# Three-block transformer layer on one core: the first attention's units one step further apart, with q, k and v copied to SBUF and norms made tile by tile

## The chip, the cores and the metric

The kernel runs on one NeuronCore of a Trainium2 chip. The core has a matrix engine (TensorE, PE in the profile), a vector engine (VectorE, DVE), an activation engine (ScalarE, ACT), a general engine (GpSimd, POOL), a queue that only starts transfers (SyncE, SP), and 16 DMA engines. SBUF is its working memory of 128 partitions; PSUM is the small memory that TensorE writes its results to, in 8 banks. Each engine runs its own instructions in order, and semaphores tie the engines together. The metric is the device time of one execution in microseconds.

## The reference

The input x has 8 batches of 512 tokens with 256 features. Four residual blocks follow one another, each on a normalised x:

```python
x = x + attn_a(layernorm(x))      # 16 heads of 64
x = x + ffn(layernorm(x))
x = x + attn_b(layernorm(x))      # 16 heads of 16, causal over the 512 tokens
x = x + ffn(layernorm(x))         # the same weights again
```

`attn_a` is unusual: it attends among the 64 channels of one head of one token, not among tokens.

```python
Q = (x @ Wq + bq).reshape(b, s, H, C) / 8;  K, V likewise
scores = einsum('bshq,bshk->bshqk', Q, K)       # 64 x 64 per token and head, causal
attn = einsum('bshqk,bshk->bshq', softmax(scores), V)
return attn.reshape(b, s, 1024) @ Wo + bo
```

So each of 4096 tokens has 16 matrices of 64 x 64 that are outer products: work for elementwise engines, not for TensorE. The FFN is silu(x W1) * (x W2), then two gelu layers of 1024, then a projection to 256; its weights are whole numbers with a scale for each output.

## The kernel before

**Groups and units.** `AttentionA` handles a group at a time: a batch b, a set g of four heads, and a tile i of 128 tokens (one token on each partition). There are 8 x 4 x 4 = 128 groups. The causal triangle of a 64 x 64 matrix is cut into squares of side 32, 16, 8, 4, 2 and 1 and the diagonal. `units` (line 549) collects the squares of a group into four units: the two heads' squares of side 32 twice, all of side 16, and all the small ones. So the first attention has 512 units, and `step(n)` (line 633) works on several at a time, each at another stage:

- `scores` (706) multiplies q by k. POOL does it for the two units of side 32, in two instructions of 1024 columns each, reading q and k from SBUF; DVE does it for the others and for the diagonal, reading q from PSUM and k from SBUF.
- `exps` (722) is the exponential on ScalarE.
- `weigh` (733) multiplies the exponentials by v on DVE, with v in PSUM, and has POOL's queue issue a DMA that adds one half of the tile to the other (line 744).
- `fold` (746) is another addition on POOL, for side 32, and the sums of the smallest squares.
- `gather` (760) reduces the rest on DVE, and POOL adds the result to `acc` (`add_rows`, 776), which holds denominators and numerators.
- `divide` (781), `turn_group` (786) and `project_out` (796) finish a group and add it to x.

Here `weigh` works on the unit of one step before `scores`, `fold` on that of two, `gather` of three steps before. Four tiles of 16 KB per partition (`wt`) carry the units. `project` (680) makes q, k and v with TensorE, two steps ahead; k and q are copied to SBUF (lines 690 and 700), and q and v stay in the two banks of `ps_qv` until the group ends.

**The rest of the layer.** `after_a` (1192) is a generator that emits FFN, second attention and FFN of a batch. Its pieces are woven into the steps of the next batch's first attention: each step emits pieces until their estimated cost has caught up (`total`, line 1235, and the loop at 1244). So the first batch's first attention has little beside it, and the last batch's remaining blocks run alone. The kernel fixes the order on PE, DVE, ScalarE and POOL itself, by the order in which it emits (`manual_schedule`). `later` and `flush` put an emission off to the next point of the same generator.

**Normalisation.** `stats` (509) takes mean and variance of several tiles on DVE, the square root on ScalarE, its reciprocal and the shift on DVE (lines 519 and 524). `normed` scales on ScalarE, and `turned_over` transposes on TensorE. For the blocks after the first attention `Normed` does three of the four tiles together and the last one later. In the FFN, line 932 takes the difference between a product and its rounded copy on POOL. In the last FFN, `fits` compares the weights with their rounded copies on DVE (line 909).

**Buffers.** `hp` has 8 blocks of 8 KB for activations, `wp` two buffers for the projection weights, which SP's queue loads, `ps_a` one bank for the first attention's other products, `ps_f` five banks for all the rest.

Of the kernel before, what the change touches and what calls it, by code (L numbers as in the profile page):

```python
# [284 lines left out]
def fast_path(ctx: ExitStack, tc: tile.TileContext, k, t, flag):  # L285

    nc = tc.nc
    ident, eps = k.ident, k.eps
# [3 lines left out]
    wp = ctx.enter_context(tc.tile_pool(name="wp", bufs=2))  # L292
# [5 lines left out]
    hp = ctx.enter_context(tc.tile_pool(name="hp", bufs=8))  # L298
    small = ctx.enter_context(tc.tile_pool(name="small", bufs=3))
    ps_qv = ctx.enter_context(tc.tile_pool(name="ps_qv", bufs=2, space=bass.MemoryType.PSUM))  # L300
    ps_a = ctx.enter_context(tc.tile_pool(name="ps_a", bufs=1, space=bass.MemoryType.PSUM))
# [24 lines left out]
    for g in range(NG):  # L326
        if g < 2:

            wqv = wp.tile([P, DC, 2 * GW], F32, tag="wqv", name=f"wqv_0_{g}")
            wk = wp.tile([P, DC, GW], F32, tag="wk", name=f"wk_0_{g}")  # L330
        else:
            both = block(f"fit_{g}")
            wqv = both[:, : DC * 2 * GW].rearrange("p (c f) -> p c f", c=DC)
            wk = both[:, DC * 2 * GW : DC * 3 * GW].rearrange("p (c f) -> p c f", c=DC)
        nc.sync.dma_start(wqv, wqv_r[:, :, g, :])
        nc.sync.dma_start(wk, wk_r[:, :, g * GW : (g + 1) * GW])
        fitted.append((wqv, wk))
# [171 lines left out]
    def stats(b, xt, part, tiles=range(NT)):  # L509

        i0, i1 = tiles[0], tiles[-1] + 1
        mv = small.tile([P, NT, 2], F32, tag=f"mv_{part}", name="mv", bufs=2)[:, i0:i1]
        for i in tiles:
            st = small.tile([P, 6], F32, tag=f"st_{part}", name="st")
            nc.vector.bn_stats(st, xt[:, i, :])
            nc.vector.bn_aggr(mv[:, i - i0, :], st)
        rstd = small.tile([P, NT], F32, tag=f"rstd_{part}", name="rstd", bufs=2)[:, i0:i1]
        nc.scalar.activation(rstd, mv[:, :, 1], AF.Sqrt, bias=eps)
        nc.vector.reciprocal(rstd, rstd)
        if part == "f":  # L520
            shift = small.tile([P, NT], F32, tag="shift", name="shift", bufs=2)[:, i0:i1]
        else:
            shift = means[:, b, 0 if part == "a" else 1, i0:i1]
        nc.vector.scalar_tensor_tensor(shift, mv[:, :, 0], -1.0, rstd, ALU.mult, ALU.mult)
        return {i: (rstd[:, i - i0 : i - i0 + 1], shift[:, i - i0 : i - i0 + 1]) for i in tiles}

    def normed(xi, rn, part):

        rstd, shift = rn
# [9 lines left out]
    def turned_over(dst, xn, pool):  # L539
# [4 lines left out]
        nc.scalar.copy(dst, pt)  # L544
# [4 lines left out]
    units = (((32, 0, 2),), ((32, 2, 2),), ((16, 0, 4),), ((8, 0, 4), (4, 0, 4), (2, 0, 4), (1, 0, 4)))  # L549
    NU = len(units)  # L550

# [10 lines left out]
    def pieces(w, n, off, nsq, cols):  # L562
# [11 lines left out]
        if n < 16:  # L574
            e, ev = (
                w[:, a * 2048 + off : a * 2048 + off + nsq * n * n].rearrange("p (x i j) -> p x i j", i=n, j=n)
# [22 lines left out]
    class AttentionA:  # L599
# [3 lines left out]
        def __init__(self):  # L603
            self.x = {0: x_first}
            self.rn, self.live = {}, {}
            self.w = {(0, g): fitted[g] for g in range(2)}
            self.wo = {}
            self.load_wo(0, 0)
            self.ready = set()
# [3 lines left out]
            self.steps = len(self.todo) + 11  # L613
# [10 lines left out]
        def load_wo(self, b, g):  # L624
            if b < NB:
                wo = wp.tile([P, GW // P, D], F32, tag="wo", name=f"wo_{b}_{g}", bufs=1)
                nc.sync.dma_start(wo, t.wo[g * GW : (g + 1) * GW].rearrange("(c p) f -> p c f", p=P))
                self.wo[b, g] = wo
# [4 lines left out]
        def step(self, n):  # L633
            b, i, g, u = self.at(n)
            if b is not None:
                self.scores(b, i, g, u)
            b, i, g, u = self.at(n + 40)
            if u == 0 and g == 0 and i == 0 and b > 0:
                self.x[b] = load_x(b)
            b, i, g, u = self.at(n + 7)  # L640
            if u == 0 and g == 0 and i == 0:
                self.rn[b] = stats(b, self.x[b], "a")
            b, i, g, u = self.at(n + 4)
            if u == 0 and g == 0:
                self.norm(b, i)
            yield
            b, i, g, u = self.at(n - 1)
            if b is not None:
                self.weigh(b, i, g, u)
            b, i, g, u = self.at(n - 2)  # L650
            if b is not None:
                self.fold(b, i, g, u)
            b, i, g, u = self.at(n + 2)
            if u == 0:
                self.project(b, i, g)
            yield
            b, i, g, u = self.at(n - 3)
            if b is not None:
                self.gather(b, i, g, u)

            b, i, g, u = self.at(n - 4)
            if u == NU - 1:
                self.divide(b, i, g)
            b, i, g, u = self.at(n - 8)
            if u == NU - 1:
                self.turn_group(b, i, g)
            b, i, g, u = self.at(n - 9)
            if u == NU - 1:
                self.project_out(b, i, g)
            yield  # L670
            b, i, g, u = self.at(n)
            if b is not None:
                self.exps(b, i, g, u)

        def norm(self, b, i):
            xnt = lnp.tile([P, DC, P], F32, tag="xnt_a", name=f"xnta_{b}_{i}", bufs=NT)
            turned_over(xnt, normed(self.x[b][:, i, :], self.rn[b][i], "a"), ps_a)
            self.live[b, i] = xnt

        def project(self, b, i, g):  # L680
# [8 lines left out]
            kt = ap_.tile([P, 2, GW], F32, tag="k", name=f"k_{u}")  # L689
            nc.scalar.copy(kt[:, 0], pk)  # L690
            qv = ps_qv.tile([P, 2, GW], F32, tag="qv", name=f"qv_{u}")
            for c in range(DC):
                nc.tensor.matmul(  # L693
                    qv.rearrange("p j f -> p (j f)"),
                    xnt[:, c, :],
                    wqv[:, c, :],
                    start=(c == 0),
                    stop=(c == DC - 1),
                )
            nc.scalar.copy(kt[:, 1], qv[:, 0])  # L700
            acc = ap_.tile([P, 2, GW], F32, tag="acc", name=f"acc_{u}", bufs=4)
            self.live[b, i, g] = (qv, kt, acc)
            if i == 1 and (b, g) != (0, 0):
                self.load_w(b + (g + 1) // NG, (g + 1) % NG)

        def scores(self, b, i, g, n_u):

            qv, kt, acc = self.live[b, i, g]
            w = wt.tile([P, 4096], F32, tag="w", name=f"w_{b}_{i}_{g}_{n_u}")
            self.live[b, i, g, n_u] = w  # L710
            if n_u == 0:
                nc.vector.tensor_tensor(acc[:, 0, :], qv[:, 0, :], kt[:, 0], ALU.mult)
            for n, off, nsq, cols in squares(units[n_u]):

                eng, q = (nc.gpsimd, kt[:, 1]) if n_u < 2 else (nc.vector, qv[:, 0])
                for e, ev, rows, columns in pieces(w, n, off, nsq, cols):
                    shape = list(e.shape)
                    eng.tensor_tensor(  # L718
                        e, rows(q).to_broadcast(shape), columns(kt[:, 0]).to_broadcast(shape), ALU.mult
                    )  # L720

        def exps(self, b, i, g, n_u):
            qv, kt, acc = self.live[b, i, g]
            w = self.live[b, i, g, n_u]
            if n_u == 0:
                nc.scalar.activation(acc[:, 0, :], acc[:, 0, :], AF.Exp, scale=C**-0.5)
            if n_u < 3:
                e = w.rearrange("p (b a r) -> p a b r", a=2, b=units[n_u][0][0] // JB)[:, 0]
            else:
                e = w[:, : sum(nsq * n * n for n, off, nsq, cols in squares(units[n_u]))]  # L730
            nc.scalar.activation(e, e, AF.Exp, scale=C**-0.5)  # L731

        def weigh(self, b, i, g, n_u):


            qv, kt, acc = self.live[b, i, g]
            w = self.live[b, i, g, n_u]
            if n_u == 0:
                nc.vector.tensor_tensor(acc[:, 1, :], acc[:, 0, :], qv[:, 1, :], ALU.mult)
            for n, off, nsq, cols in squares(units[n_u]):  # L740
                for e, ev, rows, columns in pieces(w, n, off, nsq, cols):
                    nc.vector.tensor_tensor(ev, e, columns(qv[:, 1]).to_broadcast(list(e.shape)), ALU.mult)  # L742
            if n_u < 3:
                nc.gpsimd.dma_start(w[:, :2048], w[:, 2048:], accum_op=ALU.add)  # L744

        def fold(self, b, i, g, n_u):

            qv, kt, acc = self.live[b, i, g]
            w = self.live[b, i, g, n_u]
            for n, off, nsq, cols in squares(units[n_u]):  # L750
                if n == 32:
                    nc.gpsimd.tensor_tensor(w[:, :1024], w[:, :1024], w[:, 1024:2048], ALU.add)  # L752
                if n <= 2:
                    both = w.rearrange("p (a f) -> p a f", a=2)[:, :, off : off + nsq * n * n]
                    both = both.rearrange("p a (r j) -> p a r j", j=n)
                    if n == 2:
                        nc.gpsimd.tensor_tensor(both[..., :1], both[..., :1], both[..., 1:], ALU.add)
                    self.add_rows(acc, n, cols, both[..., 0])

        def gather(self, b, i, g, n_u):  # L760

            qv, kt, acc = self.live[b, i, g]
            w = self.live.pop((b, i, g, n_u))
            for n, off, nsq, cols in squares(units[n_u]):
                if n <= 2:
                    continue
                if n >= 16:
                    both = w[:, : 2 * nsq * n * JB].rearrange("p (a r j) -> p a r j", a=2, j=JB)
                else:
                    both = w.rearrange("p (a f) -> p a f", a=2)[:, :, off : off + nsq * n * n]  # L770
                    both = both.rearrange("p a (r j) -> p a r j", j=n)
                red = ap_.tile([P, 2, nsq * n], F32, tag=f"red{nsq * n}", name=f"red_{b}_{i}_{g}_{n_u}_{n}")
                nc.vector.tensor_reduce(red, both, AX.X, ALU.add)  # L773
                self.add_rows(acc, n, cols, red)

        def add_rows(self, acc, n, cols, part):

            rows = acc[:, :, cols].rearrange("p a (x t) -> p a x t", t=2 * n)[..., n:]
            nc.gpsimd.tensor_tensor(rows, rows, part.rearrange("p a (x i) -> p a x i", i=n), ALU.add)  # L779

        def divide(self, b, i, g):
            qv, kt, acc = self.live[b, i, g]
            nc.vector.reciprocal(acc[:, 0, :], acc[:, 0, :])
# [555 lines left out]
```

## Time and profile before

| what | value |
|---|---|
| median of 3 runs | 4479.16 us (4476.88 to 4479.33) |
| the profiled execution | 4477.29 us, its span 4475.5 us |
| granted clock of TensorE, mean | 0.806 |
| ScalarE, exponentials of 2048 columns (line 731) | 384, mean 1914 ns |
| DVE, reductions of 2048 columns (line 773) | 256, mean 2277 ns |
| POOL, folds (line 752) | 256, mean 2594 ns |
| DMA, the adding transfer (line 744) | 384 of 1024 KB, 7.2 us from issue to landing |
| from 4200 us to the end | PE busy 249.8 of 275 us, DVE 82.7, POOL 31.9 |

Busy shares are means over the whole span, and the last batch's end differs from the rest. In a row of a group, the first number after the bar is its busy time in us, the second the mean of one instruction in ns, and what follows the second bar is the idle time of the engine just before these instructions, with what ended it. An instruction's duration runs from its start on the engine to its end: what it waits for on a semaphore lies outside of it, what holds it after its start lies within.

### The profile page before, as it was taken

Reading aid. Unit: us, or ns where it says so; the run is one execution under the profiler, and the core shown is the slowest. Engines: PE = TensorE matmul, PEld = TensorE weight load, DVE = VectorE, ACT = ScalarE, POOL = GpSimd, SP = SyncE. Lnnn points to the kernel's source line nnn. Section 1 sums busy time; section 2 is a strip of 40 time slices with the busy share of each in tenths; the row PEclk is TensorE's granted clock in tenths of the full one; section 3 lists DMA queues with packets and bytes.
Section 4 is the critical chain, followed back from the end, with each engine's and each line's share of the span. In section 5 each row is a group of like instructions: output and inputs, shape, how many; then the busy total and the mean of one; then the engine's idle time right before and its main releaser. Section 6 shows DMA issues by size and latency. Waiting matters only on the chain. (4 is left out here: it accounts for less than half of the span.)

```text
span 4475.5 us, 37073 instructions
## 1 busy us (share of the span) xinstructions
PE 2959.5 (66%) x11880; PEld 2017.9 (45%) x11880; DVE 3511.3 (78%) x4113; ACT 2422.0 (54%) x3068; POOL 2962.6 (66%) x2634
## 2 busy tenths in 40 slices
PE   3322277567865777757875678657777568756998
PEld 2111154245633555335642456335553356425757
DVE  5988877888888888878878788888888788787205
ACT  3333365565754765556654666547655566546332
POOL 6777776766776776767767667667767677676201
PEclk6555588788987889878987889778898789878999
DMA  7555566657755767647765577557676477655514
GB/s 234 124 123 119 123 163 168 124 140 178 192 125 111 181 165 176 134 112 177 178 168 124 139 177 198 119 111 182 161 178 133 110 180 172 168 115 135 180 43 147
DMA packets 118364, 670.24 MB, mean 150 GB/s; under 512 B 12672, under 2 KB 31883, under 8 KB 43536
## 3 DMA queue, kind: packets, MB, share of 16 engines
q0 software_dynamic: 78336, 570.46, 56.3%
q1 hardware_dynamic: 39824, 97.32, 6.3%
q8 instruction: 96, 1.57, 0.1%
q14 instruction: 108, 0.88, 0.1%
HBM read 255.12 MB, written 9.96 MB: 59 GB/s over the span
## 5 line engine op out<-in xcount | busy, mean ns | idle before, releaser
L742 DVE TENSOR_TENSOR w<-w,qv 128x1024 f32<-128x1024 f32 (+3 forms) x1280 | 1198.7, 985 | 443.5 <-ACT w L731 443.5
L731 ACT ACTIVATE w<-w 128x2048 f32<-128x2048 f32 (+1 forms) x512 | 966.0, 1887 | 842.0 <-POOL w L718 560.8
L1016 PE MATMUL ph<-h,hidden 128*128 128x512 f32 x4096 | 1095.3, 424 | 158.4 <-POOL h L932 90.4
L773 DVE TENSOR_REDUCE red<-w 128x128 f32<-128x1024 f32 (+2 forms) x640 | 1036.6, 1636 | 23.9 <-POOL w L752 19.1
L718 POOL TENSOR_TENSOR w<-k 128x1024 f32<-128x1024 f32 x512 | 1036.2, 2136 | 7.6 <-ACT k L700 7.4
L1016 PEld LDWEIGHTS ph<-h,hidden 128*128 128x128 f32 x4096 | 819.7, 203 | 386.9 <-POOL h L932 113.7
L744 POOL DMA_DIRECT2D w<-w x384 | 334.8, 872 | 979.1 <-DVE w L742 331.4
L752 POOL TENSOR_TENSOR w<-w 128x1024 f32<-128x1024 f32 x256 | 664.1, 2594 | 64.6 <-DMA w<-w 64.2
L718 DVE TENSOR_TENSOR w<-qv,k 128x1024 f32<-128x1024 f32 (+3 forms) x768 | 601.5, 838 | 6.9
L779 POOL TENSOR_TENSOR acc<-acc,red 128x256 f32<-128x256 f32 (+1 forms) x640 | 473.1, 739 | 139.5 <-DVE red L773 121.0
L948 PE MATMUL pw<-xnt,gate 128*128 128x512 f32 (+2 forms) x1152 | 328.7, 439 | 166.8 <-ACT silu L927 84.6
L543 PE MATMUL ps_ln<-ident,xn 128*128 128x128 f32 x256 | 76.5, 415 | 488.7 <-ACT xn L536 330.6
L1126 PE MATMUL pyb<-eb,vb 128*32 128x512 f32 (+3 forms) x1024 | 219.6, 525 | 255.7 <-ACT eb L1121 255.5
L948 PEld LDWEIGHTS pw<-xnt,gate 128*128 128x128 f32 x1152 | 236.6, 225 | 244.9 <-ACT silu L927 101.8
L686 PE MATMUL pk<-wk,xnta 128*128 128x256 f32 x512 | 191.6, 512 | 196.6 <-DVE x L808 195.2
L693 PE MATMUL qv<-wqv,xnta 128*128 128x512 f32 x512 | 288.0, 692 | 0.0
L543 PEld LDWEIGHTS ps_ln<-ident,xn 128*128 128x128 f32 x256 | 37.3, 193 | 529.7 <-ACT xn L536 353.7
L1041 PE MATMUL pof<-w,h 128*128 128x256 f32 x1024 | 244.9, 399 | 12.5 <-ACT h L981 12.5
L981 ACT ACTIVATE h<-ph,s_sb 128x512 fp32r<-128x512 f32 (+1 forms) x256 | 172.2, 688 | 129.7 <-PE ph L1016 128.4
L1126 PEld LDWEIGHTS pyb<-eb,vb 128*32 128x32 f32 x1024 | 66.2, 117 | 362.2 <-ACT eb L1121 336.5
L686 PEld LDWEIGHTS pk<-wk,xnta 128*128 128x128 f32 x512 | 124.1, 258 | 231.4 <-DVE x L808 206.3
L1041 PEld LDWEIGHTS pof<-w,h 128*128 128x128 f32 x1024 | 204.4, 202 | 48.0 <-ACT h L981 17.3
(130 smaller groups left out, 4196.5 us busy)
## 6 DMA issues: line engine op xcount, KB each, us to landing
w<-w POOLq DMA_DIRECT2D x384, 1024.0 KB, 7.2
hidden<-in_h POOLq DMA_DIRECT2D x128, 1024.0 KB, 6.6
gate<-in_w12p POOLq DMA_DIRECT2D x32, 1024.0 KB, 5.7
w<-w_d SPq DMA_DIRECT2D x16, 1024.0 KB
wqv<-wqv_d SPq DMA_DIRECT2D x30, 512.0 KB, 3.1
wo<-in_wo SPq DMA_DIRECT2D x32, 256.0 KB, 6.6
wbqk<-wbqk_d SPq DMA_DIRECT2D x8, 1024.0 KB
w<-in_h SPq DMA_DIRECT2D x8, 1024.0 KB, 8.5
```

The lines of the kernel that those rows point to most:

```text
L686: nc.tensor.matmul(pk, xnt[:, c, :], wk[:, c, :], start=(c == 0), stop=(c == DC - 1))
L693: nc.tensor.matmul(qv.rearrange("p j f -> p (j f)"), xnt[:, c, :], wqv[:, c, :], start=(c == 0), stop=(c == DC - 1),)
L718: eng.tensor_tensor(e, rows(q).to_broadcast(shape), columns(kt[:, 0]).to_broadcast(shape), ALU.mult)
L731: nc.scalar.activation(e, e, AF.Exp, scale=C**-0.5)
L742: nc.vector.tensor_tensor(ev, e, columns(qv[:, 1]).to_broadcast(list(e.shape)), ALU.mult)
L744: nc.gpsimd.dma_start(w[:, :2048], w[:, 2048:], accum_op=ALU.add)
L752: nc.gpsimd.tensor_tensor(w[:, :1024], w[:, :1024], w[:, 1024:2048], ALU.add)
L773: nc.vector.tensor_reduce(red, both, AX.X, ALU.add)
L779: nc.gpsimd.tensor_tensor(rows, rows, part.rearrange("p a (x i) -> p a x i", i=n), ALU.add)
L948: nc.tensor.matmul(pj[:, toks], w[:, m % 4, j, c, :], xs[:, p, c, toks], start=(p == 0 and c == 0), stop=(p == 1 and c == DC - 1),)
L1016: nc.tensor.matmul(pss[j], w[:, j, c, :], h_in(p, c), start=(p == 0 and c == 0), stop=(p == 1 and c == MC - 1),)
L1041: nc.tensor.matmul(po, h(0, c)[:, i * P : (i + 1) * P], w3[:, c, :], start=(c == 0), stop=(c == MC - 1))
```

## The change

- q, k and v of a group are copied to one SBUF tile of 3 x 256 columns (`keep_qkv`). `scores` and `weigh` read all of them there, on DVE too. `ps_qv` has one bank, `ps_a` two.
- The unit of side 16 stands between the two of side 32, so that POOL makes scores in every other step. Between its two instructions stands the adding DMA of another unit.
- `weigh` works on the unit of two steps before `scores`, `fold` of three, `gather` of four (three for the small squares). The small squares have a tile of their own (`ws`, 3840 columns), beside the four of 4096.
- Additions to `acc` are emitted in the step after their reduction; copies out of PSUM, transposes and additions to x are parted in the same way, so that they stand some pieces after what they need.
- Each tile of tokens is normalised by itself. Square root and reciprocal become a power of -0.5 on POOL, and the shift is made there too: four POOL instructions for a tile (`scales`), or for a block in the first attention. Each stage of `Normed.tile` is put off with `later`.
- `hp` has 7 blocks instead of 8; the hidden activations are split into four blocks by pairs of chunks. The projection weights have one buffer, loaded after the last tile of a group set.

```diff
-    wp = ctx.enter_context(tc.tile_pool(name="wp", bufs=2))
+    wp = ctx.enter_context(tc.tile_pool(name="wp", bufs=1))
...
-    hp = ctx.enter_context(tc.tile_pool(name="hp", bufs=8))
+    hp = ctx.enter_context(tc.tile_pool(name="hp", bufs=7))
...
-    ps_qv = ctx.enter_context(tc.tile_pool(name="ps_qv", bufs=2, space=bass.MemoryType.PSUM))
-    ps_a = ctx.enter_context(tc.tile_pool(name="ps_a", bufs=1, space=bass.MemoryType.PSUM))
+    ps_qv = ctx.enter_context(tc.tile_pool(name="ps_qv", bufs=1, space=bass.MemoryType.PSUM))
+    ps_a = ctx.enter_context(tc.tile_pool(name="ps_a", bufs=2, space=bass.MemoryType.PSUM))
...
+    def moments(xi, mv):
+
+        st = small.tile([P, 6], F32, tag="st", name="st")
+        nc.vector.bn_stats(st, xi)
+        nc.vector.bn_aggr(mv, st)
+
+    def scales(mv, rstd, shift):
+
+        nc.gpsimd.tensor_scalar(rstd, mv[:, :, 1], EPS, None, ALU.add)
+        nc.gpsimd.tensor_tensor(rstd, rstd, k.power[:, : rstd.shape[-1]], ALU.pow)
+        nc.gpsimd.tensor_tensor(shift, mv[:, :, 0], rstd, ALU.mult)
+        nc.gpsimd.tensor_scalar(shift, shift, -1.0, None, ALU.mult)
...
-    units = (((32, 0, 2),), ((32, 2, 2),), ((16, 0, 4),), ((8, 0, 4), (4, 0, 4), (2, 0, 4), (1, 0, 4)))
+    units = (((32, 0, 2),), ((16, 0, 4),), ((32, 2, 2),), ((8, 0, 4), (4, 0, 4), (2, 0, 4), (1, 0, 4)))
     NU = len(units)
+    SMALL = 1920
...
         def step(self, n):
...
+            before = self.at(n - 2)
+            if before[0] is not None:
+                self.weigh(*before)
+            unit = self.at(n)
+            on_pool = unit[3] in (0, 2)
+            if on_pool:
+                half = self.scores(*unit)
+                next(half)
+            if before[0] is not None:
+                self.halve(*before)
+            if on_pool:
+                next(half, None)
...
+            if self.at(n - 1)[0] is not None:
+                self.exps(*self.at(n - 1))
+            yield
+            if unit[0] is not None and not on_pool:
+                for _ in self.scores(*unit):
+                    pass
+            for args in self.sums:
+                self.add_rows(*args)
+            self.sums = []
...
+            b, i, g, u = self.at(n - 3)
+            if u in (0, 2):
+                self.fold(b, i, g, u)
...
+        def keep_qkv(self, b, i, g):
+            pk, qv = self.live.pop("qkv")
+            kt = ap_.tile([P, 3, GW], F32, tag="k", name=f"k_{b}_{i}_{g}")
             nc.scalar.copy(kt[:, 0], pk)
...
+            nc.scalar.copy(kt[:, 1:].rearrange("p j f -> p (j f)"), qv)
+            self.live[b, i, g] = [kt]
...
         def scores(self, b, i, g, n_u):
...
+            if n_u < NU - 1:
+                w = wt.tile([P, 4096], F32, tag="w", name=f"w_{b}_{i}_{g}_{n_u}")
+            else:
+                w = wt.tile([P, 2 * SMALL], F32, tag="ws", name=f"ws_{b}_{i}_{g}", bufs=1)
...
-                eng, q = (nc.gpsimd, kt[:, 1]) if n_u < 2 else (nc.vector, qv[:, 0])
                 for e, ev, rows, columns in pieces(w, n, off, nsq, cols):
                     shape = list(e.shape)
                     eng.tensor_tensor(
-                        e, rows(q).to_broadcast(shape), columns(kt[:, 0]).to_broadcast(shape), ALU.mult
+                        e, rows(kt[:, 1]).to_broadcast(shape), columns(kt[:, 0]).to_broadcast(shape), ALU.mult
                     )
+                    yield
...
         def weigh(self, b, i, g, n_u):
...
             if n_u == 0:
-                nc.vector.tensor_tensor(acc[:, 1, :], acc[:, 0, :], qv[:, 1, :], ALU.mult)
+                nc.vector.tensor_tensor(acc[:, 1, :], acc[:, 0, :], kt[:, 2], ALU.mult)
             for n, off, nsq, cols in squares(units[n_u]):
                 for e, ev, rows, columns in pieces(w, n, off, nsq, cols):
-                    nc.vector.tensor_tensor(ev, e, columns(qv[:, 1]).to_broadcast(list(e.shape)), ALU.mult)
-            if n_u < 3:
+                    nc.vector.tensor_tensor(ev, e, columns(kt[:, 2]).to_broadcast(list(e.shape)), ALU.mult)
+
+        def halve(self, b, i, g, n_u):
+
+            if n_u < NU - 1:
+                w = self.live[b, i, g, n_u]
                 nc.gpsimd.dma_start(w[:, :2048], w[:, 2048:], accum_op=ALU.add)
...
+        def tile(self, i):
             toks = slice(i * P, (i + 1) * P)
...
+            moments(self.xt[:, i, :], mv[:, 0, :])
+
+            def scale():
+                scales(mv, rstd, shift)
+                later(normalise)
...
-    total = 299.4
+    total = 304.8
...
-        for n in range(-7, a.steps):
+        for n in range(-9, a.steps):
```

## The prediction

> **What bounds the kernel now.** First the page, engines and slices: no engine is full, VectorE (DVE) is nearest.
>
> ```profile
> PE 2959.5 (66%) x11880; PEld 2017.9 (45%) x11880; DVE 3511.3 (78%) x4113; ACT 2422.0 (54%) x3068; POOL 2962.6 (66%) x2634
> ...
> DVE  5988877888888888878878788888888788787205
> ACT  3333365565754765556654666547655566546332
> POOL 6777776766776776767767667667767677676201
> ```
>
> The last three slices differ: the first attention is over, only the last batch's rest runs. The score halves that GpSimd (POOL) makes, two for each of 256 units, give the pace of what is before, here in the answer for line 718 (count, shortest, median and longest, first and last start):
>
> ```profile
> L718 POOL TENSOR_TENSOR w<-k x512: 1941/2209/2279, 25.2 to 4118.7; 128x1024 f32<-128x1024 f32 x171
> ```
>
> That is 4093.5 us for 128 groups (batch, projection group, token tile), 32.0 us each, and 4475.5 - 4093.5 = 382 us of start and end. Busy time in that stretch, from the table of windows:
>
> ```profile
> core 0: us, PE busy (x) PEld busy (x) DVE busy (x) ACT busy (x) POOL busy (x), PEclk, DMA share, GB/s
> 25.00:4119.00 4094.00, 2632.72 (x10363) 1776.26 (x10364) 3381.78 (x3928) 2289.11 (x2831) 2899.94 (x2557) 0.79 0.65 151
> ```
>
> A group has 3381.8 / 128 = 26.4 us of DVE and 22.7 of POOL. So DVE sets the pace, with 5.6 us of gaps. The groups by shape say which gaps:
>
> ```profile
> L742 DVE TENSOR_TENSOR w<-w,qv 128x1024 f32<-128x1024 f32 x896 | 1054.6, 1212 | 443.5 <-ACT w L731 443.5
> ...
> L718 DVE TENSOR_TENSOR w<-qv,k 128x1024 f32<-128x1024 f32 x384 | 457.5, 1219 | 6.9
> ...
> L524 DVE SCALAR_TENSOR_TENSOR shift<-mv,rstd 128x3 f32<-128x3 f32 x16 | 24.3, 1519 | 0.5
> ...
> L344 DVE TENSOR_TENSOR wqv<-wqv,last_qv 128x1024 f32<-128x1024 f32 x1 | 1.2, 1226 | 8.8 <-DMA wqv<-in_wqv 8.8
> ```
>
> 443.5 us is `weigh` waiting for the exponential of the same unit: 3.5 us a group, what the extra step of distance is aimed at. But the third row is the one to stop at. It handles three numbers per partition and takes 1519 ns in the mean; the answer for its line has the spread:
>
> ```profile
> L524 DVE SCALAR_TENSOR_TENSOR shift<-mv,rstd x32: 154/160/3789, 571.2 to 4369.7; 128x3 f32<-128x3 f32 x16, 128x1 f32<-128x1 f32 x16
> ```
>
> Its two inputs, mean and reciprocal deviation, are both in SBUF. The timeline of one long case, DVE first, then POOL:
>
> ```profile
> 1068.43 3.78 DVE L524 SCALAR_TENSOR_TENSOR shift<-mv,rstd 128x3 f32<-128x3 f32 x1
> ```
> ```profile
> 1068.08 4.10 POOL L718 TENSOR_TENSOR w<-k 128x1024 f32<-128x1024 f32 x2
> ```
>
> DVE ends at 1072.21, POOL's second score half at 1072.18. An instruction of 0.16 us lasts exactly until POOL stops. The other direction is in the last FFN, where line 909 compares two SBUF tiles:
>
> ```profile
> 4382.10 1.29 POOL L932 TENSOR_TENSOR h<-silu,h 128x512 fp32r<-128x512 f32 x1 [0.74 <-ACT h L931]
> ...
> 4383.31 2.28 DVE L909 TENSOR_TENSOR w<-w,gate 128x2048 f32<-128x2048 f32 x1
> ...
> 4384.13 2.60 POOL L932 TENSOR_TENSOR h<-silu,h 128x512 fp32r<-128x512 f32 x1 [0.74 <-ACT h L931]
> ```
>
> The same POOL instruction takes 2.60 instead of 1.29 us: 1.3 more, about what was left of line 909 when it came (until 4385.59). A DVE instruction with two SBUF inputs and a POOL `tensor_tensor` exclude each other. DVE's products of today (lines 712, 718, 739, 742) read q or v from PSUM and are free of this: line 742's longest is 1222 ns against a median of 1209.
>
> [...] the trace has 1226 (line 344, both in SBUF) against 1212 with one in PSUM. So nothing is gained per instruction.
>
> **The change part by part.**
>
> *q, k, v in SBUF.* All 20 products of a group on DVE now have two SBUF inputs. By the rows of lines 712, 718, 739 and 742 they are 1962 us, 15.3 a group; neighbours overlap (two pieces take 2.34, not 2.42), which leaves 14.7, and 20 x 14 ns of the longer form make 15.0. POOL's `tensor_tensor` rows (scores 1036, folds 664, row sums 308, 203 and 165, FFN differences 170, divisions 121, pair sums 116) are 2783 us, 21.7 a group; the window's busy time less the 440 us of DMA issues gives 19.2. I take 20.2. These two now add: 35.2 us under one lock, above the 32.0 of today, before anything is late. ScalarE's copy grows from 256 to 512 columns; it has 46% idle and hides it.
>
> *Power on GpSimd.* 8 x 12 tiles and 8 blocks, 104 calls of four POOL instructions, 416. No row shows `power` or such a small shape. From below 100 ns (the 128x1 memset), 42 us in all; from above 1 us, 416 us. The row sums take 646 ns for 128 and 801 for 256 columns, about 0.5 us with no columns; with two of the four single-input I take 0.4: 166 us, 1.3 a group, under the lock too. DVE loses some 50 us of reciprocals and shifts and ScalarE 45 table loads of 1.28 us, neither now the limit.
>
> *The distance and the fifth tile.* `weigh` takes the unit of two steps ago, so the 443.5 us go. What is late next is the lock. A group by hand, with POOL half-scores 2.0, folds 2.4, row sums 0.6 to 0.8, DMA issues 0.85, DVE pieces 1.17, reductions 2.2 or 1.15, reciprocal 1.7:
> - first step: POOL half 0 to 2.0; DVE, held, weighs 2.0 to 4.35 and makes the diagonal product to 4.75; POOL, queued behind `weigh` with its accumulating DMA, issues it to 5.2, second half to 7.2, division to 8.15; DVE's reciprocal and reduction lie beside these.
> - second: row sum to 8.75; DVE weighs the small squares and makes scores to 13.65; POOL sums and folds to 18.5, DVE's reduction beside it.
> - third: POOL half to 20.5; DVE product and `weigh` to 23.25; DMA issue and half to 26.1, row sum to 26.85; DVE's three reductions to 27.75.
> - fourth: DVE `weigh` and scores to 32.65; POOL's sums and fold to 37.15.
>
> 37.2 us, of which the lock is held some 35. Who slips in first changes the order, not the sum. POOL's FFN differences (170/128 = 1.3) and the scales (1.3) come on top, since they need the lock: 39.8. The FFN's DVE work reads PSUM and is laid under POOL's time; if that cover fails it costs up to 2.7 more a group. The first batch has no such additions: 16 x 2.6 = 42 us less.
>
> *The rest.* Seven blocks for eight, weights in one buffer (a transfer of 3.1 us with some 30 us to spare), a second bank for ps_a, tile-by-tile norms: nothing in the main stretch, where PE and SP's queue have slack. In the end stage PE is busy 250 of 275 us, so at most 25 can be won; a late block may cost as much. I take 0.
>
> Sum: 128 x 39.8 - 42 + 382 = 5434, say 5430 us. That is against the span; the profiled execution took 4477.3 and the median 4479.2, so it carries over as it is.
>
> **The rivals.**
> - The lock packs nearly without a gap: 20.2 + 15.0 + 1.3 = 36.5 a group, 128 x 36.5 + 382 = 5054. For it: either engine has hundreds of instructions to run ahead with, and the extra step leaves few waits on data. Against: `weigh` to DMA issue to fold is a chain across both engines. With every term at its low end (19.2 + 15.0 + 0.3) the floor is 4800.
> - The engines stall each other far more, DVE's reductions falling behind its blocked products: wholly in series 26.4 + 20.2 + 1.3 = 47.9, or 6513; a third of the way from the forecast, 5780, and half of it, 5950. For it: DVE works in order, and POOL's two independent halves in a row did not let it in between. Against: reductions need only follow, and POOL's dependent row sums leave gaps.
> - Faster: the lock does not bind these broadcast forms, or only for part of an instruction. Then the 3.5 us of `weigh`'s wait go and 0.3 come: 28.8 a group, 4070; with a fifth of that wait found again, 4160. It decides if products stay near 1.2 us beside POOL. For it: between the starts of the first halves of line 718 many groups already lie 27.8 us apart, where no FFN work comes between. Against: both excerpts.
> - The distance gains what the lock costs: about 4480, if 3.5 us of lock waits a group is all.
>
> **How the numbers follow.** Forecast (5200 to 5700) 0.66, tight packing 0.16, stalls 0.11, faster 0.05, even 0.02. A measurement tells 0.2%, 9 us, from no change. Faster and even are left outside the range with the floor's lowest part and the worst of the stalls: 4950 to 5850. Slower 0.93, within 0.2% 0.02, faster 0.05.
>
> **What would show it.** Right: DVE products of 128x1024 far over 1.21 us in the mean, 2 us or so, with POOL's scores and folds lengthened too; DVE busy near full while groups take about 40 us; no large idle before `weigh`. Wrong: products at 1.21 to 1.25 us beside POOL, or groups under 32 us. Small POOL instructions over 1 us would move the sum up by the power alone.

## The result, and the profile after

The changed kernel takes 5143.43 us in the median (5142.01 to 5144.86), the kernel before, run beside it, 4478.19: 1.149 times as long (95% interval 1.147 to 1.151). The profiled execution has a span of 5141.8 us. Engines and slices of its page:

```profile
PE 2967.4 (58%) x11880; PEld 2051.0 (40%) x11880; DVE 4639.1 (90%) x4001; ACT 2297.5 (45%) x2911; POOL 3748.9 (73%) x3051
...
DVE  6999999999999999999999999999999999999605
ACT  2222244445544545335544455445454355444433
POOL 7777777777777777777777777777777778777501
```

DVE works 112 instructions fewer than before and is busy 1128 us longer; POOL is busy 786 us longer. TensorE's busy time hardly changes, and ScalarE's falls by some 124 us. The groups by shape (columns as before) say which instructions grew:

```profile
L777 DVE TENSOR_TENSOR w<-w,k 128x1024 f32<-128x1024 f32 x768 | 1458.6, 1939 | 0.0
...
L774 DVE TENSOR_TENSOR acc<-acc,k 128x256 f32<-128x256 f32 x128 | 208.5, 1629 | 0.0
L743 DVE TENSOR_TENSOR acc<-k 128x256 f32<-128x256 f32 x128 | 191.4, 1495 | 8.9 <-ACT k L734 8.9
```
```profile
L753 POOL TENSOR_TENSOR w<-k 128x1024 f32<-128x1024 f32 x512 | 1216.9, 2377 | 7.7 <-ACT k L734 6.8
L788 POOL TENSOR_TENSOR w<-w 128x1024 f32<-128x1024 f32 x256 | 690.4, 2697 | 3.7 <-DMA w<-w 3.6
```

The two small products of a group in the kernel before:

```profile
L739 DVE TENSOR_TENSOR acc<-acc,qv 128x256 f32<-128x256 f32 x128 | 52.6, 411 | 13.0 <-ACT acc L726 13.0
L712 DVE TENSOR_TENSOR acc<-qv,k 128x256 f32<-128x256 f32 x128 | 47.4, 370 | 7.3 <-ACT k L700 7.3
```

Two readings. The last column of the first row is 0.0: `weigh` (now line 777) no longer waits for its exponential, the 443.5 us are gone. The mean beside it is 1939 ns for a product that took 1212. The two small products took 411 and 370 ns and take 1629 and 1495. Such a wait is not idle time in this profile (0.0 and 8.9 us before the 128 of either line): the instruction has started and is held, so it shows as a long instruction on a busy engine. Not every product is held; the answer for line 777 has the spread (count, shortest, median and longest in ns):

```profile
L777 DVE TENSOR_TENSOR w<-w,k x768: 1204/1223/3433, 33.3 to 4810.9; 128x1024 f32<-128x1024 f32 x192
```

Half of them take at most 1223 ns, against 1212 in the mean with v in PSUM, so reading SBUF by itself costs some 11 ns a product here. The start of the ninth group on the timeline (start, duration), DVE and then POOL:

```profile
321.35 2.17 DVE L743 TENSOR_TENSOR acc<-k 128x256 f32<-128x256 f32 x1
323.44 1.74 DVE L825 RECIPROCAL acc<-acc 128x256 f32<-128x256 f32 x1
...
336.05 4.11 DVE L777 TENSOR_TENSOR w<-w,k 128x1024 f32<-128x1024 f32 x2
340.08 1.21 DVE L814 TENSOR_REDUCE red<-w 128x128 f32<-128x1024 f32 x1
```
```profile
320.30 2.93 POOL L753 TENSOR_TENSOR w<-k 128x1024 f32<-128x1024 f32 x1
323.19 0.86 POOL L783 DMA_DIRECT2D w<-w  x1
...
335.80 2.14 POOL L753 TENSOR_TENSOR w<-k 128x1024 f32<-128x1024 f32 x1
340.70 0.87 POOL L783 DMA_DIRECT2D w<-w  x1 [2.77 <-DVE w L777]
```

At 321.35 the diagonal product starts and ends at 323.52, 0.29 us after POOL's half (323.23). At 336.05 two pieces of `weigh` take 4.11 instead of 2.34 us: the first stands until POOL's half ends at 337.94. POOL's DMA issue, which needs both pieces, is late by the same 1.8 us.

The pace: POOL's 512 score halves run from 24.7 to 4798.2, 37.3 us a group against 32.0. Start and end take 5141.8 - 4773.5 = 368 us, against 382. All of the loss lies in the first attention's stretch, and in every batch of it.

### The profile page after: what moved, and what is told of

It is laid out like the page before. It is cut to its first block, busy times and chain, and to the rows that moved or that the text cites. A ratio compares the mean times of both kernels' runs of the same rounds, so it can differ in the third digit from the quotient of the medians.

```text
span 5141.8 us, 37118 instructions
## 1 busy us (share of the span) xinstructions
PE 2967.4 (58%) x11880; PEld 2051.0 (40%) x11880; DVE 4639.1 (90%) x4001; ACT 2297.5 (45%) x2911; POOL 3748.9 (73%) x3051
## 5 line engine op out<-in xcount | busy, mean ns | idle before, releaser
L777 DVE TENSOR_TENSOR w<-w,k 128x1024 f32<-128x1024 f32 x768 | 1458.6, 1939 | 0.0
L753 POOL TENSOR_TENSOR w<-k 128x1024 f32<-128x1024 f32 x512 | 1216.9, 2377 | 7.7 <-ACT k L734 6.8
L767 ACT ACTIVATE w<-w 128x2048 f32<-128x2048 f32 x384 | 734.0, 1912 | 884.9 <-POOL w L753 731.3
L814 DVE TENSOR_REDUCE red<-w 128x128 f32<-128x1024 f32 (+1 forms) x384 | 595.2, 1550 | 14.1 <-POOL w L788 13.8
L837 PEld LDWEIGHTS pta<-ident,acc 128*128 128x128 f32 x256 | 37.7, 199 | 1387.9 <-POOL acc L829 1385.0
L814 DVE TENSOR_REDUCE red<-ws 128x256 f32<-128x2048 f32 (+1 forms) x256 | 445.6, 1745 | 144.1 <-POOL acc L821 144.1
L753 DVE TENSOR_TENSOR ws<-k 128x1024 f32<-128x1024 f32 (+3 forms) x512 | 445.5, 929 | 0.0
L777 DVE TENSOR_TENSOR ws<-ws,k 128x1024 f32<-128x1024 f32 (+3 forms) x512 | 438.3, 914 | 5.4 <-ACT ws L767 5.4
L767 ACT ACTIVATE ws<-ws 128x1920 f32<-128x1920 f32 x128 | 231.2, 1806 | 403.5 <-DVE ws L753 403.1
L753 DVE TENSOR_TENSOR w<-k 128x1024 f32<-128x1024 f32 x256 | 353.5, 1420 | 0.0
L821 POOL TENSOR_TENSOR acc<-acc,ws 128x256 f32<-128x256 f32 x256 | 306.0, 1195 | 20.1
```

The lines of the kernel that those rows point to most:

```text
L753: eng.tensor_tensor(e, rows(kt[:, 1]).to_broadcast(shape), columns(kt[:, 0]).to_broadcast(shape), ALU.mult)
L777: nc.vector.tensor_tensor(ev, e, columns(kt[:, 2]).to_broadcast(list(e.shape)), ALU.mult)
L814: nc.vector.tensor_reduce(red, self.columns_of(w, n, off, nsq), AX.X, ALU.add)
```

## The experiments

Twelve kernels ran. Times are medians; ratios are to the kernel before, run beside them, with 95% intervals. e1 to e8 ran on one chip, e9 to e12 on another, where the kernel before took within 0.1% of the same. The group is the distance from the first score half on POOL to the last, over 128. The sum of DVE's products is that of the durations of the 2304 multiplications of `scores` and `weigh` in each trace.

| run | edit | us | ratio | group, us | DVE's products, us |
|---|---|---|---|---|---|
| before | | 4477 to 4481 | 1 | 32.0 | 2004 |
| after | the whole change | 5143.4 | 1.149 (1.147 to 1.151) | 37.3 | 3196 |
| e1 | after, q and v from PSUM | 4206.4 | 0.939 (0.937 to 0.940) | 30.0 | 2013 |
| e2 | before, q and v from SBUF | 5521.4 | 1.232 (1.230 to 1.235) | 40.1 | 3490 |
| e3 | after, v from PSUM | 4487.4 | 1.002 (1.001 to 1.003) | 32.2 | 2456 |
| e4 | after, q from PSUM | 4765.4 | 1.064 (1.062 to 1.065) | 34.3 | 2745 |
| e5 | after, e1's banks alone | 5143.9 | 1.149 (1.147 to 1.151) | 37.3 | 3196 |
| e6 | after, norms on ScalarE and DVE | 5163.3 | 1.153 (1.151 to 1.155) | 37.5 | 3182 |
| e7 | e1, norms on ScalarE and DVE | 4295.2 | 0.960 (0.958 to 0.961) | 30.7 | 2015 |
| e8 | e1, third buffer for reductions | 4108.0 | 0.918 (0.916 to 0.919) | 29.2 | 2017 |
| e9 | after, POOL's halves together | 5223.7 | 1.167 (1.165 to 1.169) | 37.8 | 3246 |
| e10 | e1, POOL's halves together | 4341.0 | 0.970 (0.968 to 0.971) | 31.0 | 2005 |
| e11 | e7, shift with one tensor input | 4211.8 | 0.941 (0.939 to 0.942) | 30.1 | 2005 |
| e12 | e11 with e8's buffer | 4120.8 | 0.921 (0.919 to 0.922) | 29.3 | 2004 |

**Where the operands lie: e1 to e5.** The edit of e1; e3 leaves out its lines on q, e4 those on v, e5 has only the banks:

```diff
-    ps_qv = ctx.enter_context(tc.tile_pool(name="ps_qv", bufs=1, space=bass.MemoryType.PSUM))
-    ps_a = ctx.enter_context(tc.tile_pool(name="ps_a", bufs=2, space=bass.MemoryType.PSUM))
+    ps_qv = ctx.enter_context(tc.tile_pool(name="ps_qv", bufs=2, space=bass.MemoryType.PSUM))
+    ps_a = ctx.enter_context(tc.tile_pool(name="ps_a", bufs=1, space=bass.MemoryType.PSUM))
...
-            eng = nc.gpsimd if n_u in (0, 2) else nc.vector
+            eng, q = (nc.gpsimd, kt[:, 1]) if n_u in (0, 2) else (nc.vector, qp)
...
-                    nc.vector.tensor_tensor(ev, e, columns(kt[:, 2]).to_broadcast(list(e.shape)), ALU.mult)
+                    nc.vector.tensor_tensor(ev, e, columns(vp).to_broadcast(list(e.shape)), ALU.mult)
```

> The changed kernel, but DVE's products read q and v from PSUM again (two banks for them, one for the other products); POOL's scores keep their copy of q, and distance, order, fifth tile and norms stay as changed. Theory of the lock (DVE products with two SBUF inputs and POOL's tensor_tensor exclude each other): DVE's products of 1024 columns fall from 1.94 to about 1.21 us, POOL's score halves from 2.38 to 2.1, undisturbed groups from 34.8 to 28 us or less, the whole to 4050 to 4250 us, below the kernel before. Rival, the new order and the power on POOL cost the time: it stays above 4900 us, with the products at 1.21 us and new idle time in front of them.

The rows of e1 for `weigh` and POOL's halves:

```profile
L780 DVE TENSOR_TENSOR w<-w,qv 128x1024 f32<-128x1024 f32 x768 | 900.3, 1214 | 55.5 <-ACT w L769 55.5
```
```profile
L755 POOL TENSOR_TENSOR w<-k 128x1024 f32<-128x1024 f32 x512 | 1075.5, 2101 | 11.0 <-DMA x<-in_x 7.8 <-DVE red L817 2.4
```

The whole loss is gone, and with it 6% of the time before: order, distance, fifth tile and tile-by-tile norms are together a gain once the products are free. POOL's halves are back at 2101 ns, undisturbed groups at 25.9 us. The rival falls.

> The kernel before, with v copied to SBUF beside k and q, and DVE's products reading all three there; nothing else of the change (acc has three buffers and is taken at the scores, to make room). Theory of the lock: products from 1.21 to about 1.9 us, 36 to 40 us a group, 5000 to 5500 us in all. Rival, reading SBUF costs only the 14 ns per product, and the change's other parts made the loss: 4480 to 4550 us.

In e2 the operands of the kernel before are moved. `acc` is also taken later there, with three buffers instead of four; no wait for it shows in the row below. The edit of the operands:

```diff
-            nc.scalar.copy(kt[:, 1], qv[:, 0])
+            nc.scalar.copy(kt[:, 1:], qv)
...
-                eng, q = (nc.gpsimd, kt[:, 1]) if n_u < 2 else (nc.vector, qv[:, 0])
+                eng, q = (nc.gpsimd, kt[:, 1]) if n_u < 2 else (nc.vector, kt[:, 1])
...
-                    nc.vector.tensor_tensor(ev, e, columns(qv[:, 1]).to_broadcast(list(e.shape)), ALU.mult)
+                    nc.vector.tensor_tensor(ev, e, columns(kt[:, 2]).to_broadcast(list(e.shape)), ALU.mult)
```

This part alone costs 23%, more than the whole change, and slightly more than I expected. The rival falls. Its pieces of `weigh` are shorter than those of after (1680 ns against 1939), its scores of 1024 columns longer (1853 against 1420 and 1217 in two rows of 256 and 128). What is much longer is one small product, the diagonal's:

```profile
L714 DVE TENSOR_TENSOR acc<-k 128x256 f32<-128x256 f32 x128 | 661.9, 5171 | 7.5 <-ACT k L700 7.5
```

One of them, and what POOL did meanwhile:

```profile
179.75 6.25 DVE L714 TENSOR_TENSOR acc<-k 128x256 f32<-128x256 f32 x1
```
```profile
178.18 2.63 POOL L754 TENSOR_TENSOR w<-w 128x1024 f32<-128x1024 f32 x1
180.48 0.73 POOL L781 TENSOR_TENSOR acc<-acc,red 128x128 f32<-128x128 f32 x1
180.90 1.00 POOL L786 TENSOR_TENSOR acc<-acc 128x256 f32<-128x256 f32 x1
181.57 4.13 POOL L720 TENSOR_TENSOR w<-k 128x1024 f32<-128x1024 f32 x2
```

POOL ran five instructions in a row, each starting before the one ahead had ended, and the product of 0.37 us stood 6.25 us, until the last was done (185.70). In 91 of the 128 cases four whole POOL instructions passed. In after the same product never takes over 2.57 us: 191 us in all against 662. That is 471 us, more than the 378 us between e2 and after; but e2 also lacks all other parts of the change, so how these 378 us come about is not shown.

> The changed kernel with v alone read from PSUM: DVE's weighing is free, its scores (about a third of the products' time) still have two SBUF inputs. Theory of the lock: the time under it falls from 15.0 to 5.2 us of DVE a group, about 27 us with POOL's, so that DVE's own 26.4 us and the waits between set the pace again: 30 to 32 us a group, 4200 to 4500 us. Weighing falls to 1.21 us, the scores on DVE stay above 1.3. Rival: above 4900 us.

> The changed kernel with q alone read from PSUM: DVE's scores are free, its weighing keeps two SBUF inputs. Theory of the lock: 9.8 us of DVE and some 22 of POOL a group are under it, about 32 us, with gaps 33 to 35: 4600 to 4900 us, nearer to the changed kernel than the run with v in PSUM. Rival, the loss comes from the number of products that collide and not from their length: q and v help about in the same measure, 4500 to 4700 both.

The pieces of `weigh` and of the scores in e3, then in e4:

```profile
L780 DVE TENSOR_TENSOR w<-w,qv 128x1024 f32<-128x1024 f32 x768 | 898.8, 1210 | 24.5 <-ACT w L769 24.4
...
L755 DVE TENSOR_TENSOR w<-k 128x1024 f32<-128x1024 f32 x256 | 449.5, 1795 | 0.0
```
```profile
L779 DVE TENSOR_TENSOR w<-w,k 128x1024 f32<-128x1024 f32 x768 | 1269.8, 1693 | 22.4 <-ACT w L769 22.4
...
L755 DVE TENSOR_TENSOR w<-qv,k 128x1024 f32<-128x1024 f32 x256 | 299.6, 1209 | 0.0
```

Where an operand is in PSUM, its products are at 1.21 us, and the others are not (1.80 us in e3, 1.69 in e4). In the four runs of the new order (e1, e3, e4, after) the products' sum rises by 1183 us from end to end, 9.2 a group, and the group by 7.3: of each microsecond that products stand, 0.8 is paid. e4 came out as expected, and e3 in its range of time, near the upper end, with 32.2 us a group where I gave 30 to 32. The scores under the lock alone (e3) cost 2.2 us a group over e1, the longer weighing alone (e4) 4.3, both 7.3. The rival of e4, equal effects, falls.

> The changed kernel with the PSUM banks of the run with q and v in PSUM (two for q and v, one for the other products), while DVE goes on reading SBUF. Theory of the lock: the banks alone do nothing, 5100 to 5180 us. Rival, part of that run's gain came from the second bank for q and v: some 100 us below the changed kernel or more.

The banks do nothing: 5143.9 us against 5143.4. The rival falls.

**The norms: e6, e7, e11.** The edit of e6 and e7, and in e11 the last line for a single tile (the results' small tiles have four buffers each):

```diff
-        nc.gpsimd.tensor_scalar(rstd, mv[:, :, 1], EPS, None, ALU.add)
-        nc.gpsimd.tensor_tensor(rstd, rstd, k.power[:, : rstd.shape[-1]], ALU.pow)
-        nc.gpsimd.tensor_tensor(shift, mv[:, :, 0], rstd, ALU.mult)
-        nc.gpsimd.tensor_scalar(shift, shift, -1.0, None, ALU.mult)
+        nc.scalar.activation(rstd, mv[:, :, 1], AF.Sqrt, bias=k.eps)
+        nc.vector.reciprocal(rstd, rstd)
+        nc.vector.scalar_tensor_tensor(shift, mv[:, :, 0], -1.0, rstd, ALU.mult, ALU.mult)
...
+            nc.vector.tensor_scalar(shift, mv[:, :, 0], rstd, -1.0, ALU.mult, ALU.mult)
```

> The changed kernel with square root on ScalarE, reciprocal and shift on DVE again, still tile by tile (four buffers for the small results). Theory of the lock: 416 POOL instructions of 222 us leave the lock, 1.7 us a group, and DVE gets some 60 us of its own back, part of it under the lock: 4920 to 5080 us. Rival, POOL has time to spare and the power costs nothing: 5130 us or more, since DVE is the fuller engine.

> q and v in PSUM and the norms on ScalarE and DVE. With the products free of the lock DVE and the chains between engines set the pace, so that the theory expects little: 4150 to 4260 us against 4206 with the power on POOL. Rival, POOL's queue is a bound of its own: 100 us or more below 4206.

> q and v in PSUM, norms on ScalarE and DVE as in the run that took 4295 us, but the shift of a tile as tensor_scalar with one tensor input and the reciprocal deviation as scalar operand, where that run's scalar_tensor_tensor with two inputs took 1.2 to 1.6 us. If its 129 us were the lock, they fall under 30 us, and the whole goes to 4180 to 4230 us. If a scalar operand in SBUF counts as a second input, or the wait on ScalarE is what costs: 4270 to 4300 us.

Both expectations of mine for e6 and e7 were wrong: taking 416 instructions off POOL made after 20 us slower and e1 89 us slower. (e6 lies where its rival put it, at 5130 us or more.) For e7, e11 shows why: I had counted what leaves POOL and forgotten that the shift goes back to DVE with two SBUF inputs. In e6 these 96 instructions take 96 us, but what they cost there was not tried apart. First e7, then e11:

```profile
L519 DVE SCALAR_TENSOR_TENSOR shift<-mv,rstd 128x1 f32<-128x1 f32 x64 | 77.6, 1212 | 2.2
...
L519 DVE SCALAR_TENSOR_TENSOR means<-mv,rstd 128x1 f32<-128x1 f32 x32 | 51.4, 1606 | 1.1
```
```profile
L522 DVE TENSOR_SCALAR shift<-mv,rstd 128x1 f32<-128x1 f32 x64 | 13.7, 214 | 2.3
L522 DVE TENSOR_SCALAR means<-mv,rstd 128x1 f32<-128x1 f32 x32 | 6.9, 214 | 1.1
```

129 us for 96 instructions on one number per partition. With one tensor input and the other value as scalar operand they take 21 us, and 83 us of the time come back. A scalar operand in SBUF does not count as a second input here: 64 of the 96 lie wholly within a `tensor_tensor` of POOL, and none takes over 216 ns. Done so, the norms cost the same on either side: e11 and e1 differ by 0.1%, and the intervals of their ratios overlap.

**Who gets the lock: e9, e10.**

```diff
-                half = self.scores(*unit)
-                next(half)
+                for _ in self.scores(*unit):
+                    pass
             if before[0] is not None:
                 self.halve(*before)
-            if on_pool:
-                next(half, None)
```

> The changed kernel with POOL's two score halves one after the other and the adding DMA behind them, not between. In the kernel before, a DVE instruction under the lock waited through both halves, 3.78 us. Theory: the lock passes to DVE only where POOL waits, so the diagonal product (mean 1.50 us) or the first weighing piece now waits up to two halves: products of line 743 or 777 get longer by up to 2 us twice a group, and the whole 5250 to 5500 us. Rival, the lock passes at every instruction's end: 5143 us within 30, or less for the sake of fewer changes of hands.

> The same edit in the kernel with q and v in PSUM, where DVE's products need no lock. Here only the DMA is issued up to 2 us later: 4190 to 4260 us against 4206. If the edit costs the same here as in the changed kernel, its cost is that delay and not the lock.

My theory of e9 falls, and so does its rival in the number it named. The time is 26 us below my range, and for another reason than the lock: pieces of `weigh` take 1.96 us in the mean against 1.94, the diagonal product 1.69 against 1.50, and the edit costs more where no lock matters, 135 us in e10 against 80. For e10 itself I had named 4190 to 4260 us; I had put the delay too low. The row of folds in e10, where e1 had 147.8 us of idle time:

```profile
L789 POOL TENSOR_TENSOR w<-w 128x1024 f32<-128x1024 f32 x256 | 607.2, 2372 | 339.7 <-DMA w<-w 339.6
```

The adding DMA is issued later, so the fold waits for it. Putting the DMA issue between the halves pays by itself. In e9 POOL's second half follows the first at once, and still a waiting product of DVE comes in between in 182 of 256 pairs of halves, and waits through both in 19; in e2 it comes in between in 109 and waits through both in 123. So the DMA issue between the halves is not what keeps the diagonal product of after short: in e9 it takes at most 2.56 us. When exactly a run of POOL instructions keeps DVE out, as in e2, and when it does not, these runs do not settle.

**The buffer: e8, e12.** In e1 DVE stood 205.8 us before the last reduction of the small squares, released by POOL's addition of an earlier result:

```profile
L817 DVE TENSOR_REDUCE red<-ws 128x256 f32<-128x1024 f32 x128 | 156.0, 1219 | 205.8 <-POOL acc L824 205.8
```

Three results of the same size share two buffers there. v's copy in SBUF is not needed in e1 and makes room for a third:

```diff
-            kt = ap_.tile([P, 3, GW], F32, tag="k", name=f"k_{b}_{i}_{g}")
+            kt = ap_.tile([P, 2, GW], F32, tag="k", name=f"k_{b}_{i}_{g}")
...
-                    red = ap_.tile([P, 2, nsq * n], F32, tag=f"red{nsq * n}", name=f"red_{b}_{i}_{g}_{n_u}_{n}")
+                    red = ap_.tile([P, 2, nsq * n], F32, tag=f"red{nsq * n}", name=f"red_{b}_{i}_{g}_{n_u}_{n}", bufs=3)
```

> q and v in PSUM, v no longer copied to SBUF, and the room used for a third buffer of each reduction's result. In the run with two, DVE stood 206 us before the small squares' reduction until POOL had added an earlier result. If that is the buffer, most of it goes: 4000 to 4130 us. If POOL's lateness only shows at the next wait instead (DVE's wait for the fold was 63 us), 4170 to 4210 us.

> The same with three buffers for each reduction's result and without v's copy. If POOL's power (about 110 us there in all) is a burden on the version of 4108 us, this is the fastest: 4060 to 4100 us. If DVE's extra small instructions weigh as much, 4100 to 4130 us.

The reductions of e8:

```profile
L817 DVE TENSOR_REDUCE red<-w 128x128 f32<-128x1024 f32 x256 | 306.7, 1198 | 83.6 <-POOL w L791 83.3 <-issue 0.2
...
L817 DVE TENSOR_REDUCE red<-ws 128x256 f32<-128x1024 f32 x128 | 155.0, 1211 | 0.0
```

205.8 us become 0.0; some of it shows again at the fold (62.8 to 83.3) and elsewhere, and 98 us remain as a gain. (ScalarE's copy is shorter in e8 too, and was not tried alone.) At 4108 us, e8 beats the kernel before by 8.2% and after by 20%. e12 brings nothing more: at 4121 us, the second of its two cases came out.

## Why the prediction was right, and where it was off

The forecast was 5430 us, slower, in a range of 4950 to 5850; measured were 5143. Direction and mechanism came true. The band of 5200 to 5700, which had most of the chance, did not: the time lies below it.

- **The lock** is the name here for what the traces show: a DVE product with two SBUF inputs and a POOL `tensor_tensor` hold each other up (1939 and 2377 ns in after, 1214 and 2101 in e1, where one of the product's inputs is in PSUM). It was what decided: e1, e3 and e4 take it away whole or in part, e2 adds it to the kernel before, which becomes 23% slower with q and v read from SBUF. That it would bind all the products of a group was my estimate; the trace before had two cases (3.78 us for 0.16 on DVE, 2.60 for 1.29 on POOL). The foretold products of "2 us or so" are 1.94, and DVE at 90% without gains matches "busy near full".
- **The group by hand, 37.2 us without the FFN, is the step that was too large.** Undisturbed groups of after (most of the first batch's, from the fifth on) repeat at 34.8 us. By hand the lock is held for 35.0 us of a group and free for 2.2. In the sixth to twelfth groups of e1, where DVE's products are not held, these take 14.6 us a group and POOL's `tensor_tensor` 19.1, what overlaps on one engine counted once: 33.6 together, so the lengths by hand were 1.4 too long. In the same groups of after the lock is held or waited for in 32.2 us, another 1.4 less, and free for 2.7, a little more than by hand. Most of the second 1.4 can be laid to the changes of hands. The diagonal product takes 0.41 us when nothing holds it; the 78 that stand behind a POOL instruction in after end 0.28 us after that instruction's recorded end, so 0.13 us of their own length fall into the wait. In these groups 10 of 18 products stand; if each saves as much, that is 1.3 us a group, an estimate. Whether DVE is let in before the recorded end, or has its own start behind it by then, the lengths do not tell.
- **Slips in the sums:** a group has 18 products on DVE, not 20, which hardly touches the 15.0 us. A third and half of the way from 5430 to 6513 are 5791 and 5972, not 5780 and 5950. "Who slips in first changes the order, not the sum" is not borne out by the durations: the same products, in e2's order, last 293 us longer than in after.
- **FFN and scales, 2.6 us a group:** later batches have 37.7 us against 34.8, so 2.9. That the numbers agree may be luck: the same difference is 4.8 us in the kernel before and 4.5 in e1, where the products are free of the lock, so it holds other costs of the FFN too. The scales' 416 instructions take 222 us in after instead of my 166, but partly because they are held too: the power on one column takes 568 ns in the mean in e1 and 856 in after.
- **Start and end**, taken at 382 us, are 368. With 37.3 a group: 128 x 37.3 + 368 = 5142.
- **The rival of tight packing** (36.5 a group, 5054 us) was nearer than the forecast: 0.8 us a group off, against 2.5.
- **The distance** was sized too high for this change. I wrote that without the lock the group would go to 28.8 us, 4070 to 4160 in all. e1 has 30.0 and 4206, though `weigh` waits 76.7 us there instead of 443.5. A buffer that is one too few is part of it: e8, which mends that, is at 29.2 and 4108. What the distance alone gains was not tried apart from the order, the fifth tile and the norms.
- **That the rest costs nothing** is shown for the banks (e5). Order, seven blocks and single weight buffers were not tried one by one; e1 is faster with them, but a small cost could hide in its gain.

## What to carry to other kernels

Where the durations are like those here (fp32 products of 1939 ns in after with both inputs in SBUF, of 1214 in e1 with one in PSUM), count a DVE instruction with two SBUF inputs and a GpSimd `tensor_tensor` as work of one engine; if their sum is above the present pace (35.2 us a group as I estimated it here, against 32.0), leave one operand in PSUM, or, where it is one number per partition, make it a scalar operand (214 ns in e11, against 1212 and 1606 in e7). Even below the pace it can cost: I put e3's sum at 27 us a group, and e3 still took 2.2 us a group more than e1. Look for this in the durations and not in the idle times: a small instruction that usually takes 0.16 us and sometimes 3.8 is the sign, and it was in the profile before the change. When a wait is gone, look at the new release of the engine, for a buffer that was enough before may be the next one.

## What the runs showed of the hardware that was not expected

- DVE was kept out by several GpSimd instructions in a row, and not only by one: 6.25 us behind five of them in the lines above, 8.16 at most in e2, and in the kernel before 3.79 us behind two. It is no rule: in e9 a waiting product came in between two such instructions in 182 of 256 pairs.
- A wait behind the lock cost some 0.13 us less than the recorded lengths say: in after, 78 diagonal products of 0.41 us end 0.28 us after the recorded end of the GpSimd instruction that held them.
- A per-partition scalar operand in SBUF did not make DVE stand (e11), where the same value as a tensor input did (e7): 214 against 1212 and 1606 ns.
